# Last mixture of experts: each expert's slots past the first 256 under a branch on its token count

## The chip, the cores and the metric

The kernel runs on one core of one Trainium2 chip. A core has a matrix engine (PE, with its weight loads shown apart as PEld), a vector engine (DVE), a scalar engine (ACT), a general engine (POOL) and a queue engine (SP) that only issues transfers. Each engine runs its own instruction stream in order; the streams meet at semaphores. The metric is device microseconds of one execution, lower is better, as the median of three runs.

## The reference, cut to what matters

The model is four layers of graph attention or convolution, each followed by a feed-forward block, over 2708 nodes of 256 features. Only the last feed-forward block is touched. It is a switch-style mixture: every token goes to one of eight experts, an expert has a capacity of 424 slots, and tokens past the capacity are dropped.

```python
CAPACITY_FACTOR = 1.25
T = B * L                                   # 2708
C = max(1, math.ceil(CAPACITY_FACTOR * T / E))   # 424, E = 8
...
idx = jnp.argmax(probs, axis=-1)
pos = (jnp.cumsum(one_hot, axis=0) * one_hot).sum(-1).astype(jnp.int32) - 1
kept = pos < C
buf = jnp.zeros((E, C, D), dtype=h.dtype).at[idx, pos_safe].set(x, mode='drop')
hmid = jax.nn.relu(jnp.einsum('ecd,edf->ecf', buf, w1) + b1[:, None, :])
ybuf = jnp.einsum('ecf,efd->ecd', hmid, w2) + b2[:, None, :]
y_tok = ybuf[idx, pos_g] * (prb * kept)[:, None]
y = jnp.nan_to_num(y, nan=0.0, posinf=10000.0, neginf=-10000.0)
```

The slots of an expert are filled from 0 upwards in token order, so an expert with 211 tokens has slots 0 to 210 filled and 211 to 423 empty.

## The kernel before, in words

The kernel computes the four layers one after the other. Its last stage is the class `Switch`. While the last attention runs, `chunk` and `rank` compute the gate, each token's expert and its slot; `rank` is run in two parts, and `self.sofar` holds on every partition how many tokens each expert has got so far. `slots` then makes three tables from the slot numbers, each 128 partitions by 32 columns (8 experts times 4 tiles of 128 slots): `idg`, the row to fetch for a slot (row 0, which holds zeros, where the slot is empty), `ids`, the row to write (beyond the bounds where the slot is empty, so that nothing is written), and `prob`.

`experts` does the work, expert by expert:

- `gather` (L4749) fetches the expert's rows on POOL's queue by four indirect transfers into `xe`: 128, 128, 128 and 40 slots. Three `xe` buffers, so gathers run up to two experts ahead.
- SP loads `w1t` (L4767), `b1t`, `w2t` (L4771) and `b2t`, 2 MB of weights for each expert, into two sets of buffers.
- PE transposes `xe` in 128-column blocks into PSUM (`xt_ps`, L4778), and DVE (L99) and ACT (L101) in turn copy one half each to `xT`.
- PE computes the hidden layer for all 424 slots, in eight blocks of 128 hidden units (`h_ps`, L4788, three PSUM buffers); ACT adds the bias and applies the ReLU into `hT` (L4795). Every matmul is f32 and appears as two records in the trace.
- PE computes the output of each of the four tiles of slots (`y_ps`, L4800, eight hidden blocks, three PSUM buffers).
- DVE takes each output tile through nine operations (L4809 to L4818): bias, probability, three masks, three predicated copies for the NaN rule, and the residual.
- POOL writes the tile's rows to `out` by an indirect transfer (L4819).

The order of the instructions on each engine is made by the tile framework's scheduler from this program. It places the transposes of the next expert after the output tiles of the present one. After the last expert, `model` branches on `general` (L4956): a slow general path over the whole model that is taken only if the fast path met data that it can't treat. One branch of that kind stands in the third layer too (L4347), around a whole expert that may be unused; it is read on every engine from a one-element tile `used`. Where such a branch is not entered, each engine goes to a short second block which advances the semaphores by what the body would have given.

Of the kernel before, what the change touches and what calls it, by code (L numbers as in the profile page):

```python
# [8 lines left out]
F32 = mybir.dt.float32  # L9
I32 = mybir.dt.int32  # L10
U32 = mybir.dt.uint32
BF16 = mybir.dt.bfloat16
AF = mybir.ActivationFunctionType
ALU = mybir.AluOpType
# [4 lines left out]
N = 2708  # L19
D = 256  # L20
# [2864 lines left out]
class Route:  # L2885
# [10 lines left out]
    E = 8  # L2896
# [1114 lines left out]
class Deal:  # L4011
# [7 lines left out]
    T = (3, 2)  # L4019
# [415 lines left out]
class Switch:  # L4435
# [8 lines left out]
    E, HD, CAP = 8, 1024, 424  # L4444
    T = (CAP + 127) // 128
    S = E * T
    PARTS = 5

    def __init__(self, k, ctx, w, out, most):

        nc, tc = k.nc, k.tc
        E, S, T = self.E, self.S, self.T
        self.k, self.w, self.out, self.most = k, w, out, most
        keep = ctx.enter_context(tc.tile_pool(name="s3", bufs=1))
        self.dram = ctx.enter_context(tc.tile_pool(name="s3d", bufs=1, space=DRAM))
        self.fd = self.dram.tile([N + 1, 2 * D], F32, name="fd")
        self.idg = keep.tile([128, S], I32, name="idg")
        self.ids = keep.tile([128, S], I32, name="ids")
        self.prob = keep.tile([128, S], F32, name="prob")
        self.front = ExitStack()  # L4460
        pool = self.front.enter_context(tc.tile_pool(name="s3f", bufs=1))
        self.tmp = self.front.enter_context(tc.tile_pool(name="s3t", bufs=2))
        self.one = self.front.enter_context(tc.tile_pool(name="s3o", bufs=1))
        ps = self.front.enter_context(tc.tile_pool(name="ps_s3", bufs=1, space=PSUM))
        misc = ps.tile([128, 512], F32, name="misc_ps")
        n = self.PARTS * S
        self.id_ps = misc[:, :n]
        self.gl_ps = [misc[:, n + 32 * i : n + 32 * (i + 1)] for i in range(2)]
        n += 64
        self.tot_ps = misc[:, n : n + most * E]  # L4470
        self.in_ps = misc[:, n + most * E : n + 2 * most * E]
        assert n + 2 * most * E <= 512
        self.wg = pool.tile([128, 2, E], F32, name="wg")
        nc.sync.dma_start(self.wg, w["gate_w"].rearrange("(k p) e -> p k e", p=128))
        self.bg = pool.tile([128, E], F32, name="bg")
        nc.sync.dma_start(self.bg, brow(w["gate_b"], E))
        zero = pool.tile([1, 2 * D], F32, name="zero")
        nc.gpsimd.memset(zero, 0.0)
        nc.gpsimd.dma_start(self.fd[0:1, :], zero)
        self.lg = pool.tile([128, NT, E], F32, name="lg")  # L4480
        nc.gpsimd.memset(self.lg, 0.0)

        def count(name, n, step, **kw):
            t = pool.tile([128, n], F32, name=name)
            nc.gpsimd.iota(
                t,
                [[step, n]],
                channel_multiplier=kw.get("mult", 0),
                base=kw.get("base", 0),
                allow_small_or_imprecise_dtypes=True,  # L4490
            )
# [19 lines left out]
        self.every = pool.tile([128, 128], F32, name="every")  # L4511
        nc.gpsimd.memset(self.every, 1.0)
        self.later = pool.tile([128, E, most], F32, name="later")
        nc.gpsimd.memset(self.later, 1.0)
        nc.gpsimd.memset(self.later[:, :, 0:1], 0.0)

        self.valid = pool.tile([128, NT], F32, name="valid")
        nc.vector.tensor_scalar(self.valid, self.own, float(N), None, ALU.is_lt)
        self.p1 = pool.tile([128, 1], F32, name="p1")
        nc.vector.tensor_scalar(self.p1, self.own[:, 0:1], 1.0, None, ALU.add)  # L4520
        self.slot_f = pool.tile([128, 1 + self.PARTS, S], F32, name="slot_f")
        self.sofar = pool.tile([128, E], F32, name="sofar")
        nc.vector.memset(self.sofar, 0.0)
# [185 lines left out]
    def slots(self):  # L4709

        nc, S = self.k.nc, self.S
# [8 lines left out]
        v.tensor_copy(self.ids, idf)  # L4720
        v.tensor_tensor(self.prob, f[:, 3, :], f[:, 4, :], ALU.add)
        v.tensor_tensor(self.prob, self.prob, f[:, 5, :], ALU.add)
        self.front.close()

    def experts(self):
# [6 lines left out]
        with ExitStack() as ctx:  # L4732
# [25 lines left out]
                    )  # L4758
                return xe

            nxt = gather(0)
            for e in range(E):
                xe = nxt
                if e + 1 < E:
                    nxt = gather(e + 1)
                w1t = wp.tile([128, 2, HD], F32, name="w1t")
                nc.sync.dma_start(w1t, w["w1"][e].rearrange("(k p) h -> p k h", p=128))  # L4767
                b1t = wp.tile([128, M], F32, name="b1t")
# [2 lines left out]
                nc.sync.dma_start(w2t, w["w2"][e].rearrange("(m p) d -> p m d", p=128))  # L4771
                b2t = wp.tile([128, D], F32, name="b2t")
                nc.sync.dma_start(b2t, brow(w["b2"][e], D))
                xT = dp.tile([128, 2, CAP], F32, name="xT")
                for kk in range(2):
                    tp = pst.tile([128, CAP], F32, name="xt_ps")
                    for i, (o, n) in enumerate(tiles):
                        nc.tensor.transpose(  # L4778
                            tp[:, o : o + n],
                            xe[:n, i, kk * 128 : (kk + 1) * 128],  # L4780
                            k.ident[:n, :n],
                        )
                    k.copy(xT[:, kk, :], tp)
                hT = dp.tile([128, M, CAP], F32, name="hT")
                for m in range(M):
                    hp = ps1.tile([128, CAP], F32, name="h_ps")
                    for kk in range(2):
                        nc.tensor.matmul(  # L4788
                            hp,
                            lhsT=w1t[:, kk, m * 128 : (m + 1) * 128],  # L4790
                            rhs=xT[:, kk, :],
                            start=(kk == 0),
                            stop=(kk == 1),
                        )
                    nc.scalar.activation(hT[:, m, :], hp, AF.Relu, bias=b1t[:, m : m + 1])  # L4795
                for i, (o, n) in enumerate(tiles):
                    c = e * T + i
                    y = ps2.tile([128, D], F32, name="y_ps")
                    for m in range(M):
                        nc.tensor.matmul(  # L4800
                            y[:n],
                            lhsT=hT[:, m, o : o + n],
                            rhs=w2t[:, m, :],
                            start=(m == 0),
                            stop=(m == M - 1),
                        )

                    g = op.tile([128, D], F32, name="g")
                    nc.vector.tensor_tensor(g[:n], y[:n], b2t[:n], ALU.add)  # L4809
                    nc.vector.tensor_scalar(g[:n], g[:n], prob[:n, c : c + 1], None, ALU.mult)  # L4810
                    big = 3.4028234e38
                    mask = op.tile([128, 3, D], I32, name="mask")
                    nc.vector.tensor_tensor(mask[:n, 0, :], g[:n], g[:n], ALU.not_equal)
                    nc.vector.tensor_scalar(mask[:n, 1, :], g[:n], big, None, ALU.is_gt)
                    nc.vector.tensor_scalar(mask[:n, 2, :], g[:n], -big, None, ALU.is_lt)
                    for q in range(3):
                        nc.vector.copy_predicated(g[:n], mask[:n, q, :], sub[:n, q, :])
                    nc.vector.tensor_tensor(g[:n], g[:n], xe[:n, i, D:], ALU.add)  # L4818
                    nc.gpsimd.indirect_dma_start(  # L4819
                        out=out,  # L4820
                        out_offset=bass.IndirectOffsetOnAxis(
                            ap=ids[:n, c : c + 1], axis=0
                        ),
                        in_=g[:n],
                        in_offset=None,
                        bounds_check=N - 1,
                        oob_is_err=False,
                    )


def any_model(tc, I, out):
# [175 lines left out]
```

## Time and profile before

| | us |
|---|---|
| median of three runs (2376.36 to 2380.46) | 2378.51 |
| the profiled execution's own time | 2375.75 |
| span of the profiled execution | 2374.0 |
| PE busy in the span | 2225.6 (94%) |
| DVE busy in the span | 1537.0 (65%) |
| ACT busy in the span | 701.4 (30%) |
| POOL busy in the span | 423.3 (18%) |

The groups of instructions of the last stage, by line, between 2121 us and the end (busy time of the group, number of records):

| line | engine, what | records | busy us |
|---|---|---|---|
| L4788 | PE, hidden layer, 128x424 | 256 | 95.7 |
| L4800 | PE, output, 128 slots by 256 | 384 | 84.2 |
| L4800 | PE, output, 40 slots by 256 | 128 | 29.2 |
| L4778 | PE, transposes, 128 and 40 rows | 64 | 14.0 |
| L4795 | ACT, bias and ReLU, 128x424 | 64 | 39.3 |
| L4749 | POOL, gathers | 32 | 32.4 |
| L4819 | POOL, scatters | 32 | 31.8 |

The time that is compared is that of whole executions; the trace is one execution. Busy time of PE is the sum of matmul records, whose ends are modelled; how long a stage lasts is better read from where its first records start.

### The profile page before, as it was taken

How to read it: one execution, taken by the hardware profiler on the slowest of the kernel's cores; microseconds unless marked ns; L12 is line 12 of the kernel's file. 1: busy time of each engine (PE TensorE's matmuls, PEld its weight loads, DVE VectorE, ACT ScalarE, POOL GpSimd, SP SyncE). 2: the span in 40 equal slices, each digit the busy share in tenths (PEclk: the TensorE clock that was granted, in tenths of full speed). 3: DMA queues.
4: the chain of work that ended last, by engine and by line, in shares of the span. 5: the costliest groups of instructions: out<-in, count | busy, mean ns of one | idle time of the engine just before them, and what ended most of it. 6: DMA issues, size and time to landing. Idle time of an engine off the chain costs nothing. (4 is left out here: it accounts for less than half of the span.)

```text
span 2374.0 us, 32068 instructions
## 1 busy us (share of the span) xinstructions
PE 2225.6 (94%) x11600; PEld 1486.7 (63%) x11600; DVE 1537.0 (65%) x3478; ACT 701.4 (30%) x1469; POOL 423.3 (18%) x451
## 2 busy tenths in 40 slices
PE   7999999988899999999879998999999999959996
PEld 4777765577778767777668886667632333326664
DVE  7588887745676656655665646363589998844444
ACT  6433333213656222221150103134541211211220
POOL 1100013003100134556300010523100000012321
PEclk9999999969999999999989996999999999979998
DMA  5244332110657144333245554113133433323330
GB/s 152 67 113 114 111 85 84 38 38 12 220 158 227 42 128 100 77 83 54 31 151 150 149 165 90 23 52 97 43 97 107 114 113 102 87 101 130 125 117 15
DMA packets 168113, 235.25 MB, mean 99 GB/s; under 512 B 32126, under 2 KB 101476, under 8 KB 167941
## 3 DMA queue, kind: packets, MB, share of 16 engines
q1 hardware_dynamic: 130320, 184.03, 26.9%
q0 software_dynamic: 18688, 32.97, 6.2%
q10 hardware_dynamic: 18932, 16.05, 2.1%
q8 instruction: 96, 1.57, 0.3%
q14 instruction: 77, 0.62, 0.1%
HBM read 200.31 MB, written 33.74 MB: 99 GB/s over the span
## 5 line engine op out<-in xcount | busy, mean ns | idle before, releaser
L3551 DVE SCALAR_TENSOR_TENSOR PT<-Rr,Q,aj 128x512 f32<-128x512 f32 (+3 forms) x630 | 395.5, 680 | 103.9 <-PE acc_ps L3650 79.6
L3725 PE MATMUL acc_ps<-PT,V 128*64 128x512 f32 (+4 forms) x2016 | 333.7, 551 | 0.0
L3725 PEld LDWEIGHTS acc_ps<-PT,V 128*64 128x64 f32 (+1 forms) x2016 | 94.2, 123 | 210.2 <-issue 159.1
L1845 PE MATMUL acc_ps<-fa,PT 128*128 128x257 f32 x882 | 215.4, 383 | 1.2 <-DVE out L1865 1.2
L1845 PEld LDWEIGHTS acc_ps<-fa,PT 128*128 128x128 f32 x882 | 164.0, 190 | 66.4 <-issue 33.8
L3650 PE MATMUL acc_ps<-V,PT 128*128 128x257 f32 x882 | 196.6, 384 | 1.7 <-issue 1.6
L3650 PEld LDWEIGHTS acc_ps<-V,PT 128*128 128x128 f32 x882 | 167.9, 192 | 29.3 <-issue 2.5
L3305 PE MATMUL h_ps<-xT,w1t 128*128 128x384 f32 x512 | 176.9, 499 | 3.5 <-ACT xT L3296 3.5
L3322 PE MATMUL y_ps<-w2t,hT 128*128 128x256 f32 x768 | 169.8, 380 | 0.0
L2512 PE MATMUL acc_ps<-V,at 128*128 128x257 bf16 x1323 | 158.3, 278 | 9.2 <-DVE at L2503 7.4
L3322 PEld LDWEIGHTS y_ps<-w2t,hT 128*128 128x128 f32 x768 | 145.0, 190 | 21.0
L2512 PEld LDWEIGHTS <-at 128*128 128x128 bf16 x1323 | 129.6, 100 | 33.0 <-issue 5.2
L3305 PEld LDWEIGHTS h_ps<-xT,w1t 128*128 128x128 f32 x512 | 96.1, 193 | 68.3 <-ACT xT L3296 8.5
L1817 ACT ACTIVATE PT<-s_ps,rq 128x512 f32<-128x512 f32 (+1 forms) x126 | 79.5, 636 | 174.4 <-PE s_ps L1793 168.8
L3334 POOL DMA_INDIRECT acc<-ys,ids x48 | 91.7, 1911 | 156.9 <-DVE ys L3331 125.3
L1793 PE MATMUL s_ps<-KT,QT 128*128 128x512 f32 (+1 forms) x252 | 116.2, 548 | 2.5 <-ACT PT L1817 1.6
L1818 DVE SCALAR_TENSOR_TENSOR PT<-aj,PT 128x512 f32<-128x512 int32 (+1 forms) x126 | 79.2, 633 | 57.8 <-ACT PT L1817 57.5
L3004 POOL DMA_INDIRECT xe<-fd,idg x48 | 79.6, 1659 | 195.6 <-DVE early_f L3035 181.2
L4800 PE MATMUL y_ps<-w2t,hT 128*128 128x256 f32 (+1 forms) x512 | 112.8, 380 | 0.0
L3330 DVE TENSOR_TENSOR ys<-y_ps,b2t 128x256 f32<-128x256 f32 x48 | 20.3, 423 | 136.4 <-PE y_ps L3322 136.4
L3312 ACT ACTIVATE hT<-h_ps,b1t 128x384 f32<-128x384 f32 x128 | 74.2, 580 | 115.3 <-PE h_ps L3305 115.3
L4749 POOL DMA_INDIRECT xe<-fd,idg x32 | 32.4, 1013 | 411.4 <-DVE ids L4720 402.1
(795 smaller groups left out, 3538.8 us busy)
## 6 DMA issues: line engine op xcount, KB each, us to landing
aj<-in_adjT SPq DMA_DIRECT2D x399, 256.0 KB, 2.7
w1t<-in_L_ffn_W SPq DMA_DIRECT2D x8, 1024.0 KB, 5.2
w2t<-in_L_ffn_W SPq DMA_DIRECT2D x8, 1024.0 KB, 5.8
w1t<-in_L_ffn_w SPq DMA_DIRECT2D x8, 1024.0 KB, 6.9
w2t<-in_L_ffn_w SPq DMA_DIRECT2D x8, 1024.0 KB, 5.6
fd<-fa ACTq DMA_DIRECT2D x13, 512.0 KB, 3.1
aj<-in_adjT SPq DMA_DIRECT2D x63, 74.0 KB, 2.1
aj<-in_adjT SPq DMA_DIRECT2D x21, 202.0 KB, 2.4
```

The costliest lines, as they stand in the source:

```text
L1793: nc.tensor.matmul(s[:, :cs], lhsT=QT[:, j * 128 : j * 128 + 128], rhs=KT[:, c0 : c0 + cs], start=True, stop=True,)
L1817: nc.scalar.activation(PT[p, :n], s[p, :n], AF.Exp, scale=r)
L1845: nc.tensor.matmul(ac, lhsT=PT[:, o : o + n], rhs=fa[:, j, :], start=j == 0, stop=False)
L2512: nc.tensor.matmul(ac[:, c:], lhsT=at[:, o : o + n], rhs=V[:, j, r], start=j == 0 and q == 0, stop=False, skip_group_check=True,)
L3004: nc.gpsimd.indirect_dma_start(out=xe[:, i, :], out_offset=None, in_=self.fd[:rows, :], in_offset=bass.IndirectOffsetOnAxis(ap=idx[:, i : ...
L3305: nc.tensor.matmul(hp, lhsT=w1t[:, kk, m * 128 : (m + 1) * 128], rhs=self.xT[:, kk, :], start=(kk == 0), stop=(kk == 1),)
L3322: nc.tensor.matmul(y, lhsT=self.hT[:, m, i * 128 : (i + 1) * 128], rhs=w2t[:, m, :], start=(m == 0), stop=(m == M - 1),)
L3334: add = nc.gpsimd.indirect_dma_start(out=acc, out_offset=bass.IndirectOffsetOnAxis(ap=self.ids[:, i : i + 1], axis=0), in_=ys, in_offset=None,
L3551: nc.vector.scalar_tensor_tensor(PT, R, Q, aj, ALU.max, ALU.mult)
L3650: nc.tensor.matmul(ac[:n], lhsT=PT[:, o : o + n], rhs=V[:, j, 0, :], start=(j == 0), stop=False,)
L3725: nc.tensor.matmul(w.pop("out"), **w)
L4800: nc.tensor.matmul(y[:n], lhsT=hT[:, m, o : o + n], rhs=w2t[:, m, :], start=(m == 0), stop=(m == M - 1),)
```

## The change

Expert `e`'s work is split by slot tiles into `ahead` (tiles 0 and 1, 256 slots) and `rest` (tiles 2 and 3, 168 slots). Transposes, hidden layer and outputs of `ahead` run always. The hidden layer and the outputs of `rest` stand under a branch that is entered if the expert has more than 256 tokens. The counts are compared once for all experts, in `slots`. All four tiles are still gathered and transposed, and all weights are loaded. The flag of the branch is the count's comparison plus a number that is always zero, computed from the finished first output tile, so that it exists only once that tile is through DVE.

```diff
+    FIRST = 2
...
+        self.more = keep.tile([128, E], F32, name="more")
...
+        v.tensor_scalar(self.more, self.sofar, 128.0 * self.FIRST, None, ALU.is_gt)
         self.front.close()
...
-            nxt = gather(0)
-            for e in range(E):
-                xe = nxt
-                if e + 1 < E:
-                    nxt = gather(e + 1)
+            def load(e):
...
+            def turn(xe, xT, ts):
+                o0, o1 = ts[0][1], ts[-1][1] + ts[-1][2]
                 for kk in range(2):
-                    tp = pst.tile([128, CAP], F32, name="xt_ps")
-                    for i, (o, n) in enumerate(tiles):
+                    tp = pst.tile([128, 256], F32, name="xt_ps")
+                    for i, o, n in ts:
...
-                    k.copy(xT[:, kk, :], tp)
+                    k.copy(xT[:, kk, o0:o1], tp[:, : o1 - o0])
+
+            def up(wt, xT, hT, ts):
...
                 for m in range(M):
-                    hp = ps1.tile([128, CAP], F32, name="h_ps")
+                    hp = ps1.tile([128, 256], F32, name="h_ps")[:, : o1 - o0]
...
+            def down(e, wt, xe, hT, i, o, n):
...
+            ts = [(i, o, n) for i, (o, n) in enumerate(tiles)]
+            ahead, rest = ts[: self.FIRST], ts[self.FIRST :]
+
+            def begin(e):
+                xe, wt = gather(e), load(e)
+                return xe, wt, dp.tile([128, 2, CAP], F32, name="xT")
+
+            nxt = begin(0)
+            turn(nxt[0], nxt[2], ahead)
+            for e in range(E):
+                xe, wt, xT = nxt
+                hT = dp.tile([128, M, CAP], F32, name="hT")
+                up(wt, xT, hT, ahead)
+                turn(xe, xT, rest)
+                if e + 1 < E:
+                    nxt = begin(e + 1)
+                    turn(nxt[0], nxt[2], ahead)
+                used = op.tile([1, 1], I32, name="used")
+                for i, o, n in ahead:
+                    g = down(e, wt, xe, hT, i, o, n)
+                    if i == 0:
+
+                        no = op.tile([1, 1], F32, name="no")
+                        nc.vector.tensor_tensor(no, g[:1, :1], g[:1, :1], ALU.is_lt)
+                        nc.vector.tensor_tensor(
+                            used, self.more[:1, e : e + 1], no, ALU.add
                         )
+                with tc.If(nc.values_load(used, min_val=0, max_val=1)):
+                    up(wt, xT, hT, rest)
+                    for i, o, n in rest:
+                        down(e, wt, xe, hT, i, o, n)
```

`up` and `down` hold the loops of before (hidden layer with its activation; output tile with its nine DVE operations and its scatter), over the tiles that they are given.

More of the change, by code (lines that the diff above doesn't have):

```diff
@@ L4773, in experts @@
                 nc.sync.dma_start(b2t, brow(w["b2"][e], D))
-                xT = dp.tile([128, 2, CAP], F32, name="xT")
+                return w1t, b1t, w2t, b2t
+            def turn(xe, xT, ts):
+                o0, o1 = ts[0][1], ts[-1][1] + ts[-1][2]
                 for kk in range(2):
-                    tp = pst.tile([128, CAP], F32, name="xt_ps")
-                    for i, (o, n) in enumerate(tiles):
+                    tp = pst.tile([128, 256], F32, name="xt_ps")
+                    for i, o, n in ts:
                         nc.tensor.transpose(
-                            tp[:, o : o + n],
+                            tp[:, o - o0 : o - o0 + n],
                             xe[:n, i, kk * 128 : (kk + 1) * 128],
@@ L4782, in experts @@
                         )
-                    k.copy(xT[:, kk, :], tp)
-                hT = dp.tile([128, M, CAP], F32, name="hT")
+                    k.copy(xT[:, kk, o0:o1], tp[:, : o1 - o0])
+            def up(wt, xT, hT, ts):
+                w1t, b1t, _, _ = wt
+                o0, o1 = ts[0][1], ts[-1][1] + ts[-1][2]
                 for m in range(M):
-                    hp = ps1.tile([128, CAP], F32, name="h_ps")
+                    hp = ps1.tile([128, 256], F32, name="h_ps")[:, : o1 - o0]
                     for kk in range(2):
@@ L4790, in experts @@
                             lhsT=w1t[:, kk, m * 128 : (m + 1) * 128],
[L4791 removed]
+                            rhs=xT[:, kk, o0:o1],
                             start=(kk == 0),
@@ L4794, in experts @@
                         )
[L4795 to L4805, printed above, removed]
-                        )
[L4808 to L4828, printed above, removed]
@@ new lines, in up @@
+                    nc.scalar.activation(
+                        hT[:, m, o0:o1], hp, AF.Relu, bias=b1t[:, m : m + 1]
+                    )
+            def down(e, wt, xe, hT, i, o, n):
+                _, _, w2t, b2t = wt
+                c = e * T + i
+                y = ps2.tile([128, D], F32, name="y_ps")
+                for m in range(M):
+                    nc.tensor.matmul(
+                        y[:n],
+                        lhsT=hT[:, m, o : o + n],
+                        rhs=w2t[:, m, :],
+                        start=(m == 0),
+                        stop=(m == M - 1),
+                    )
+                g = op.tile([128, D], F32, name="g")
+                nc.vector.tensor_tensor(g[:n], y[:n], b2t[:n], ALU.add)
+                nc.vector.tensor_scalar(g[:n], g[:n], prob[:n, c : c + 1], None, ALU.mult)
+                big = 3.4028234e38
+                mask = op.tile([128, 3, D], I32, name="mask")
+                nc.vector.tensor_tensor(mask[:n, 0, :], g[:n], g[:n], ALU.not_equal)
+                nc.vector.tensor_scalar(mask[:n, 1, :], g[:n], big, None, ALU.is_gt)
+                nc.vector.tensor_scalar(mask[:n, 2, :], g[:n], -big, None, ALU.is_lt)
+                for q in range(3):
+                    nc.vector.copy_predicated(g[:n], mask[:n, q, :], sub[:n, q, :])
+                nc.vector.tensor_tensor(g[:n], g[:n], xe[:n, i, D:], ALU.add)
+                nc.gpsimd.indirect_dma_start(
+                    out=out,
+                    out_offset=bass.IndirectOffsetOnAxis(ap=ids[:n, c : c + 1], axis=0),
+                    in_=g[:n],
+                    in_offset=None,
+                    bounds_check=N - 1,
+                    oob_is_err=False,
+                )
+                return g
```

## The prediction

> **What bounds the kernel now.** I read the page's engine table first (PE busy 94%), then the stage that the change touches: the table by stretches of the last 253 us, the chain that ended last, the timeline, then the transfers. Stretch table (length; busy us and count of PE, PEld, DVE, ACT, POOL; clock; DMA share; GB/s), one expert and the end:
>
> ```profile
> 2193.00:2220.00 27.00, 26.90 (x106) 17.78 (x105) 13.73 (x38) 5.42 (x9) 8.00 (x9) 1.00 0.40 126
> 2355.00:2374.00 19.00, 0.00 (x0) 0.00 (x0) 2.66 (x8) 0.00 (x0) 2.14 (x2) 0.56 0.02 7
> ```
>
> PE fills the expert's 27 us; DVE is half idle, DMA 40% busy. The chain (start, length) repeats one pattern for each expert:
>
> ```profile
> 2193.61 11.65 PE h_ps L4788 x32
> 2205.26 13.94 PE y_ps L4800 x64
> 2219.20 0.68 PE xt_ps L4778 x4
> 2219.97 0.61 DVE xT L99
> 2220.62 11.65 PE h_ps L4788 x32
> ```
>
> So an expert lasts 2220.62 - 2193.61 = 27.01 us, of it 1.42 from the last output to the next hidden layer. What PE drops here comes off the end one for one, as long as nothing else becomes late. The first expert lasts longer (2137.27 to 2166.60 = 29.33), since its hidden layer takes 14.10 us after an idle stretch at clock 0.50. Durations that I need (timeline):
>
> ```profile
> 2178.09 14.10 PE L4800 MATMUL y_ps<-w2t,hT 128*128 128x256 f32 x64
> 2181.74 0.42 DVE L4809 TENSOR_TENSOR g<-y_ps,b2t 128x256 f32<-128x256 f32 x1 [11.92 <-PE y_ps L4800]
> 2185.25 0.42 DVE L4809 TENSOR_TENSOR g<-y_ps,b2t 128x256 f32<-128x256 f32 x1
> 1685.30 2.18 PE L4261 MATMUL h_ps<-fT,w1t 128*128 128x148 f32 x16
> ```
>
> A 256-column record costs 14.10/64 = 0.220 us, one output tile (16 records) 3.52; a 148-column record with the same weight size 0.136; DVE takes a tile through in about 3.55.
>
> **Which experts skip.** The trace tells: a scatter of tile 2 moves bytes only for filled slots. These are the software queue's lines (packets, MB, share of the engines) in the stretches in which tile 2 of experts 0, 1 and 3 was written:
>
> ```profile
> q0 software_dynamic: 48, 0.00, 0.4%
> ...
> q0 software_dynamic: 48, 0.04, 2.1%
> ...
> q0 software_dynamic: 48, 0.13, 6.5%
> ```
>
> 0.13 MB is a full tile (128 rows of 1 KB). The same view gives 0.00 for experts 2 and 4 as well, 0.13 for 5 and 6, and 0.07 for 7. So experts 0, 2 and 4 have nothing past slot 255: three of eight skip.
>
> **What a branch costs.** The kernel has two already. L4347 and L4956 are both not entered (min/median/max ns):
>
> ```profile
> L4347 PEldq TENSOR_LOAD <-used x1: 487/487/487, 1578.4 to 1578.4; - x1
> L4347 PEldq COMPARE_BRANCH  x1: 3670/3670/3670, 1579.0 to 1579.0; - x1
> L4347 ACTq COMPARE_BRANCH  x1: 50/50/50, 1574.9 to 1574.9; - x1
> L4347 DVEq COMPARE_BRANCH  x1: 72/72/72, 1581.8 to 1581.8; - x1
> L4956 PEldq COMPARE_BRANCH  x1: 3637/3637/3637, 2351.1 to 2351.1; - x1
> L4956 POOLq INC_SWDGE_SEM  x1: 2087/2087/2087, 2362.9 to 2362.9; - x1
> 1582.84 0.30 PE L4361 MATMUL xt_ps<-ident,xe 128*128 128x128 f32 x1 [2.08 <-PEq L4347]
> ```
>
> PE's jump costs 3.65 us where it passes over much code (by L4347's shapes 22 token tiles, over 1,000 PE instructions); ACT and DVE, passing over some 48, pay 0.05 to 0.07. The register load at 1578.4 ran while PE was still in the outputs (to 1580.5): the sequencer works ahead of the array.
>
> [...] here 2.08 us of idleness at 1582 left the next matmuls at full speed, and the first expert shows the slow start.
>
> **The change, part by part.** From the changed program's instruction order and the semaphores that each instruction names. t is time from the first hidden matmul of an expert.
>
> Always: hidden layer of 256 slots, 32 x 0.220 = 7.05; two output tiles 7.05; t = 14.10. Then PE's transposes: four for the next expert's tiles 2 and 3, and four for tiles 0 and 1 of the one after that. (The scheduler runs transposes one expert further ahead, so the next hidden layer never waits for a copy behind the branch.) First four: 4 x 0.174 (8 took 1.39) = 0.70. The others wait for ACT's and DVE's copies out of the two `xt_ps` buffers. DVE: tile 0 arrives at 10.6, done at 14.3; `no` 0.14 (the 1x1 `used` at L4008 took 0.14); first operation of tile 1, 0.42; `used`, about 15.1; its copy to 15.45. So PE ends its transposes near 16.1, against 15.5 without these waits. The register load starts when the last transpose is handed over: 15.75 + 0.49 = 16.2, branch 0.05.
>
> Not entered: the second block's semaphore step and jump, 0.2 (at L4347 the matmul followed 0.17 after the branch): next expert at 16.5. Saves 27.0 - 16.5 = 10.5 each for experts 2 and 4. DVE still finishes tile 1 (to 18.5) and POOL its 2.09 us semaphore step; both lie under the next expert's 14 us before anyone asks for them.
>
> Entered: hidden layer of 168 slots, 32 records; by columns 0.141 (424 take 0.356), floor 0.136; I take 0.148: 4.73; outputs 7.05. 16.35 + 4.73 + 7.05 = 28.15, so +1.15 each for 1, 3, 5. DVE's tail of tile 3 is covered: the next `h_ps` buffers wait for ACT alone, and ACT's first copy waits for PE only. If that cover failed it would cost up to 3.6 each.
>
> Ends: expert 0: 7.05 + 2.72 (slow start, 14.10 - 32 x 0.356) + 0.70 (four transposes before its outputs) + 7.05 + 2.4 + 0.25 (five semaphore waits of 0.05 ahead of the first branch) = 20.2: saves 9.1. Expert 6 has four transposes fewer: +0.55. Expert 7 has none, but PE waits for `used`: branch over at 15.7, outputs end at 27.5 against 25.6: +1.9. `more` is one DVE operation of 128x8, 0.17, before the first gather: +0.1.
>
> Sum: -9.1 - 21.0 + 3.45 + 0.55 + 1.9 + 0.1 = **-24.1**. Profiled execution 2375.75 becomes 2351.7; it lies 2.8 under the median shown, so the median becomes **2354.4**.
>
> Moved queues: SP's load of the expert two on is now issued after the branch, when PE has freed the buffers: near the start of the expert before it. Landing took 6.5 to 6.9 (w1t), 5.6 (w2t), together some 12, against 16.5: hidden. POOL's gather for the expert two on comes after the branch too: from t = 5.2 (after a skip, behind its 2.09) or 7.5 (after an entered branch, behind a scatter that waits for the landing of the one before, 5.9 at most). Its second tile is asked for at 15.4, issued at 6.5 or 8.8; gathers landed in 4.4 in the median, some 7 in the loaded start: about 2 spare, costing nothing.
>
> **Unknown: PE's short jump.** The body is 32 matmuls of the program, 128 PE instructions with weight loads. No jump of that size on PE is in the trace. Below: 0.05 as on ACT; above: 3.65, plus up to 2.7 if the clock drops. I take 0.05[...]; a gain is excluded. The range keeps the other end.
>
> **Rivals.**
> - *Skips refetch on PE* (22%): one to three of the skips cost 3.65: 2358 to 2365, with the clock 2373. For: both PE jumps in the trace cost it. Against: both were far.
> - *Late gathers* (4%): PE waits at the transposes; a landing of 10 us gives five waits of 1 to 3.4: near 2364.
> - *Every branch refetches, entered or not* (6%), the slower side: place, PE at all eight branches; price 3.65 each, 29.2 - 24.1 = +5.1: 2383.6, more if the clock drops. It decides from 3.0 us per branch. Against: L4347's final jump within PE's code cost 0.17 with its semaphore step.
> - *Flag always set* (3%): no skip, eight entered: 1.15 x 6 + 0.55 + 1.9 + 0.4 = +9.7: 2388. Against: `sofar` is complete before `slots`, and the trace shows three experts at or under 256.
>
> **How the numbers follow.** Likeliest as worked out: 60%, 2350 to 2359 with the terms' spread; 5% stays for other causes. 0.2% (4.8 us) is what this measurement can tell. Faster: 60 + 22 + 4 and 2 of the rest, 88%. Within: 3%. Slower: 6 + 3, 9%. Range 2349 to 2367: from three us better terms to three skips with a refetch and some more.
>
> **What would show it.** Hidden-layer starts 16.5 us apart after experts 2 and 4 and 28.2 after 1, 3 and 5; 160 records of the 168-column hidden layer, five experts' worth; PE's compare-and-branch under 0.1 us. Wrong if these branches read 3.6, if PE idles over 1 us at a transpose for `xe`, or if 256 such records appear.

## The result, and the profile after

| | before | after |
|---|---|---|
| median, us | 2378.10 (2376.36 to 2380.46) | 2341.39 (2338.96 to 2347.69) |
| profiled execution, us | 2375.75 | 2339.33 |
| its span, us | 2374.0 | 2337.5 |

The ratio is 0.9849, with a 95% interval of 0.9826 to 0.9872: faster by 36.7 us, where 24 were forecast and the range ended at 29.5. (The kernel before has four runs here; the table ahead of the prediction had three of them, with the median 2378.51.) The direction and the mechanism were right, the size was not. Three experts skip their branch, that is, PE jumps over its body, as was read from the bytes of the scatters. The groups by line and shape of the last stage (records, then busy us, mean ns, idle time before them and its releasers) have 160 hidden-layer records of 168 columns, five experts' worth:

```profile
L4793 PE MATMUL h_ps<-xT,w1t 128*128 128x256 f32 x256 | 59.8, 394 | 1.8 <-PEq L4865 1.8
L4793 PE MATMUL h_ps<-xT,w1t 128*128 128x168 f32 x160 | 24.1, 309 | 1.9 <-DVE g L4819 1.9
```

The table by stretches (length; busy us and count of PE, PEld, DVE, ACT, POOL; clock; DMA share; GB/s), for expert 2 (skips), expert 3 (enters), and from the last output to the end:

```profile
2177.45:2193.75 16.30, 15.48 (x74) 13.08 (x73) 9.09 (x29) 4.21 (x10) 7.01 (x7) 1.00 0.45 132
2193.75:2221.23 27.48, 27.09 (x137) 22.33 (x137) 12.44 (x35) 7.79 (x19) 7.09 (x7) 1.00 0.50 168
...
2319.46:2337.50 18.04, 0.00 (x1) 0.00 (x0) 3.35 (x10) 0.00 (x0) 1.91 (x2) 0.60 0.02 7
```

PE still bounds an expert: 15.48 of 16.30 us busy in a skipped one. The chain that ended last (start, length) through expert 5, which enters, has a copy by ACT in the middle of the transposes, where a copy by DVE stood behind them before:

```profile
2237.51 7.15 PE h_ps L4793 x32
2244.66 6.91 PE y_ps L4809 x32
2251.57 0.75 PE xt_ps L4780 x4
2252.34 0.31 ACT xT L101
2252.69 0.66 PE xt_ps L4780 x4
2253.35 4.70 PE h_ps L4793 x32
2258.05 7.03 PE y_ps L4809 x32
2265.08 7.10 PE h_ps L4793 x32
```

No branch stands in this chain: PE's second hidden layer follows the transposes at once. Where a branch does cost, the timeline shows it as idle time before the instruction that follows (in brackets, with the releaser). First the skip of expert 2, then the entry of expert 7, which has no transposes to fill the wait:

```profile
2192.66 0.66 PE L4780 MATMUL xt_ps<-ident,xe 128*128 128x128 f32 x4 [0.39 <-ACT xT L101]
2193.75 2.61 PE L4793 MATMUL h_ps<-xT,w1t 128*128 128x256 f32 x11 [0.43 <-PEq L4865]
...
2307.61 4.68 PE L4793 MATMUL h_ps<-xT,w1t 128*128 128x168 f32 x31 [1.33 <-DVE g L4819]
```

The branch's own instructions on PE at expert 2 (ns, then start) show a jump of 0.36 us; the general branch after the last expert took 3.64 us before and 3.74 after:

```profile
L4865 PEldq TENSOR_LOAD <-used x1: 304/304/304, 2192.7 to 2192.7; - x1
L4865 PEldq COMPARE_BRANCH  x1: 364/364/364, 2193.1 to 2193.1; - x1
```

The prediction took everything ahead of the first hidden matmul as unchanged. It isn't. These are PE's timelines of the start, first before, then after:

```profile
2133.19 0.43 PE L4778 MATMUL xt_ps<-ident,xe 40*128 40x40 f32 x2 [0.24 <-DMA xe<-fd,idg]
2136.72 0.45 PE L4778 MATMUL xt_ps<-ident,xe 128*128 128x128 f32 x1 [3.10 <-DMA xe<-fd,idg]
2137.27 3.17 PE L4788 MATMUL h_ps<-xT,w1t 128*128 128x424 f32 x4
```

```profile
2124.44 0.66 PE L4780 MATMUL xt_ps<-ident,xe 128*128 128x128 f32 x2 [7.12 <-DMA xe<-fd,idg]
2127.02 0.69 PE L4780 MATMUL xt_ps<-ident,xe 128*128 128x128 f32 x2 [1.92 <-DMA xe<-fd,idg]
2129.12 1.02 PE L4780 MATMUL xt_ps<-ident,xe 128*128 128x128 f32 x4 [1.41 <-DMA xe<-fd,idg]
2130.12 3.33 PE L4793 MATMUL h_ps<-xT,w1t 128*128 128x256 f32 x7
```

Before, a ninth transpose stands ahead of expert 0's hidden layer, and it waits 3.10 us for a gather: it is expert 1's. So the order described for the kernel before, in which the next expert's transposes follow the outputs, does not hold for this one. After, it stands behind the hidden layer. From the first gather (2121.85 before, 2118.23 after) to the first hidden matmul it is 15.42 us before and 11.89 after.

To see which part belongs to the change, each trace is cut at four points: first gather, first hidden matmul, end of the last output, end of the span. (An expert's period, below, is the time from its first hidden matmul to that of the next expert, for the last one to the end of its outputs.) The experiments give two more traces of the changed kernel and one more of the kernel before (us; the last column is the position of the first gather):

| kernel | start | experts | end | sum | first gather |
|---|---|---|---|---|---|
| before | 15.42 | 216.99 | 19.74 | 252.15 | 2121.85 |
| before again (e8) | 14.90 | 217.37 | 19.82 | 252.09 | 2119.71 |
| after | 11.89 | 189.34 | 18.04 | 219.27 | 2118.23 |
| after again (e1) | 12.16 | 188.71 | 18.14 | 219.01 | 2152.49 |
| after, third (e9) | 12.50 | 188.40 | 18.21 | 219.11 | 2143.49 |
| no branch (e3) | 12.34 | 216.18 | 19.38 | 247.90 | 2154.30 |
| all entered (e5) | 12.69 | 222.97 | 18.37 | 254.03 | 2120.97 |

The sums repeat within 0.3 us, so the change is worth 252.1 - 219.1 = 33.0 us: about 3.0 at the start, 28.4 in the experts, 1.65 at the end. The other 3.6 us between the two profiled executions lie ahead of the first gather, where the programs' work is the same but for the comparison of the counts, 0.16 us on DVE.

### The profile page after: what moved, and what is told of

Its sections match the earlier page's. It is cut to its first block, busy times and chain, and to the rows that moved or that the text cites. A ratio compares the mean times of both kernels' runs of the same rounds, so it can differ in the third digit from the quotient of the medians.

```text
span 2337.5 us, 32378 instructions
## 1 busy us (share of the span) xinstructions
PE 2188.8 (94%) x11664; PEld 1493.0 (64%) x11664; DVE 1519.2 (65%) x3449; ACT 709.3 (30%) x1517; POOL 417.5 (18%) x445
## 3 DMA queue, kind: packets, MB, share of 16 engines
q1 hardware_dynamic: 130320, 184.03, 27.5%
## 5 line engine op out<-in xcount | busy, mean ns | idle before, releaser
L4278 PE MATMUL y_ps<-w2t,hT 128*128 128x256 f32 (+1 forms) x432 | 99.5, 379 | 0.0
```

The source lines that it names most:

```text
L4278: last = nc.tensor.matmul(y[:n], lhsT=hT[:, m, o : o + n], rhs=wts[e][1][:, m, :], start=(m == 0), stop=(m == M - 1),)
```

## The experiments

Runs sent together share a chip and its runs of the kernel before, so ratios are compared, not microseconds: on the chip of e1 to e4 and that of e9 to e12 the kernel before took 2405 to 2406, on that of e5 to e8 2375.5.

**e1: the changed kernel again.**

> The changed kernel as it is, once more. Theory: of the 36.5 us between the two profiles only the stage from its first gather to its last output belongs to the change (about 31: 27.6 in the experts' periods, 3.4 in the start of expert 0); the 3.6 us by which the first gather came earlier and the 2 us after the last output are this execution's own. Then in this trace first gather to first hidden matmul is 11.9, first hidden matmul to the end of the outputs 189.3, each within 0.4, while the first gather may stand anywhere between 2118 and 2124, and five rounds give a gain of 29 to 35. Rival: the change makes the untouched stages faster, by where the code lies; then the first gather stands at 2118.2 again, within 0.7, and the gain is 36 to 37.

Measured: 2371.62 against 2405.06, ratio 0.9861 (0.9844 to 0.9878), 33.4 us. Start 12.16, experts 188.71 (expected 189.3 within 0.4, so 0.2 beyond). The first gather stood at 2152.49, far outside the expected window, because this chip is slower as a whole, so the expectation's test by position says nothing. But e1 and e4, whose work ahead of it is the same, differ there by 4.4 us on one chip. So the 3.6 us can be an execution's own, and the sum of the stage agrees with the measured gain. The shorter end, which the expectation took for chance, was there again (18.14): it belongs to the program.

**e2: the kernel before, with expert 1's transposes behind expert 0's hidden layer.**

```diff
-                            k.ident[:n, :n],
+                            (late if e == 1 else k.ident)[:n, :n],
...
+                if e == 0:
+                    late = dp.tile([128, 128], F32, name="late")
+                    no = op.tile([128, 1], F32, name="no")
+                    nc.vector.tensor_tensor(no, hT[:, M - 1, :1], hT[:, M - 1, :1], ALU.is_lt)
+                    nc.vector.tensor_scalar(late, k.ident, no, None, ALU.add)
```

> The kernel before, with expert 1's transposes made to follow expert 0's hidden layer (two small vector operations give their identity matrix a dependence on it). Theory: in the kernel before one transpose of expert 1, which waits for its gather, stands ahead of expert 0's hidden layer and holds it for 3.1 us; then first gather to first hidden matmul falls from 15.4 to 12.0 to 12.3, all later periods stay at 27.0, expert 0's at 29.3 to 29.6, and the time falls by 3 (ratio 0.9987). Rival: the landing of the first weights (15.2 us in the table of transfers) holds the hidden layer; then 15.2 to 15.4 stays and the time is unchanged.

Measured: ratio 0.9990 (0.9981 to 0.9999); start 13.10, where 12.0 to 12.3 was expected. From the timeline:

```profile
2164.86 0.43 PE L4778 MATMUL xt_ps<-ident,xe 40*128 40x40 f32 x2 [0.49 <-DMA xe<-fd,idg]
2165.38 0.51 ACT L101 COPY xT<-xt_ps 128x424 f32<-128x424 f32 x1 [22.42 <-PE xt_ps L4778]
2165.93 14.58 PE L4788 MATMUL h_ps<-xT,w1t 128*128 128x424 f32 x32 [0.63 <-issue]
```

The hidden layer no longer waits for expert 1, and not for its weights either: it starts as the second copy to `xT` ends (2165.89). The start fell by 1.8 to 2.3 of the 3 us. Most of what is left is the gap of 0.63 after the last transpose, in which the 424-column copies run. With the split hidden layer this gap is gone: it needs only tiles 0 and 1, which are copied while tiles 2 and 3 are transposed. Expert 0's period rose to 29.87, so the stage gained 2.1 in sum.

**e3: the split without a branch.**

```diff
-                with tc.If(nc.values_load(used, min_val=0, max_val=1)):
-                    up(wt, xT, hT, rest)
-                    for i, o, n in rest:
-                        down(e, wt, xe, hT, i, o, n)
+                up(wt, xT, hT, rest)
+                for i, o, n in rest:
+                    down(e, wt, xe, hT, i, o, n)
```

> The changed kernel with the rest of each expert's slots run always, with no branch and no flag in the program. Theory: the start is as in the changed kernel (11.9), splitting the hidden layer costs 0.1 to 0.2 for each expert, so periods of 27.1 to 27.3 and expert 0 at 29.3; in all 1 to 3 us under the kernel before (2375 to 2377). Rival: the start in the changed kernel came from the branch (its queue of semaphores or the moved transfers), then it is 15.4 here and the time is 1 above before; or the split hidden layer is what costs the 0.5 of an entered expert, then periods are 27.5.

Measured: 2403.77 against 2405.06, ratio 0.9990 (0.9981 to 0.9998); by the trace 4.2 us under the kernel before from the first gather on. Start 12.34: the start's gain needs the split and the order, not a branch. The periods of experts 1 to 6 are 26.96 to 26.98, no longer than before (27.01): splitting a hidden layer of 424 columns into 256 and 168 costs next to nothing (from its first record to the next step's, 7.01 and 4.56 us here, 11.49 in one). Expert 0 took 27.74 instead of 29.3 to 29.7, and expert 7 26.60 instead of 25.59: four transposes lie in expert 0's period instead of seven, and four in expert 7's instead of none. The timeline shows how the transposes lie here:

```profile
2201.39 0.90 PE L4780 MATMUL xt_ps<-ident,xe 128*128 128x128 f32 x4
2202.22 0.70 PE L4809 MATMUL y_ps<-w2t,hT 128*128 128x256 f32 x2
2202.75 0.60 PE L4780 MATMUL xt_ps<-ident,xe 128*128 128x128 f32 x4
2203.19 6.64 PE L4809 MATMUL y_ps<-w2t,hT 128*128 128x256 f32 x30
```

**e4: the flag without its wait.**

```diff
+            flags = [
+                nc.values_load(self.more[:1, e : e + 1], min_val=0, max_val=1)
+                for e in range(E)
+            ]
...
-                with tc.If(nc.values_load(used, min_val=0, max_val=1)):
+                with tc.If(flags[e]):
```

`more` becomes an integer table, and `no` and `used` go. The scheduler still places each register load right ahead of its branch.

> The changed kernel with the flag read straight from the table of counts, without the number that waits for the finished first output tile. Theory: that wait costs only where no transposes stand behind the outputs, at expert 7 (1.3 us of idle PE ahead of its second hidden layer); that one goes to 0.1 or less, skips stay at 16.3 and entered experts at 27.5, in all 1.2 under the changed kernel. Rival: PE's wait at all branches is for the flag; then skips fall to 15.9, entered experts to 27.3, expert 0 by 0.7, and the sum is 3 to 4.

Measured: ratio 0.9858 (0.9843 to 0.9873). Skips 16.32 and 16.29, entered 27.48 to 27.50: no change there. Expert 7 fell from 27.26 to 25.67 and expert 6 from 27.20 to 26.53. The second hidden layer of expert 7 starts without a wait:

```profile
2335.15 4.72 PE L4793 MATMUL h_ps<-xT,w1t 128*128 128x168 f32 x32
```

So the wait for the flag cost 1.6 + 0.7 = 2.3 us, where few or no transposes stand between the outputs and the branch; I had missed expert 6. As whole runs, 1.6 us between e4 and e1 is within their spread.

**e5: all experts enter.**

```diff
-        v.tensor_scalar(self.more, self.sofar, 128.0 * self.FIRST, None, ALU.is_gt)
+        v.tensor_scalar(self.more, self.sofar, -1.0, None, ALU.is_gt)
```

> The changed kernel with the comparison always true (counts over minus one), so that all eight experts take the branch. Theory: an entered branch costs 0.5 against the same program without it (27.5 against 26.97 between hidden layers), expert 7 0.7 and expert 0 about 2 (its branch has five more semaphore waits); experts 0, 2 and 4 rise by 11.2 each over the changed kernel, so the stage from the first hidden matmul to the last output lasts 222 (216.2 without a branch, 188.7 in the changed kernel), and against the kernel before the time is within 2 us of no change: plus 5 in the stage, minus 3.3 at its start, minus 1.7 after its last output. Rival: the whole gain is not in the skipped work but in the new order and start; then this stays 10 or more under the kernel before.

Measured: 2378.07 against 2375.5, ratio 1.0007 (0.9998 to 1.0016); experts 222.97. Periods: 30.82 for expert 0, 27.52 to 27.56 for experts 1 to 5, 27.20 for 6, and 27.26 for 7. With nothing to skip the change gains nothing. Against e3 the eight branches, with the order of the transposes that goes with them, cost 222.97 - 216.18 = 6.8 us.

**e6: a second branch, around tile 3.** On the kernel of e4:

```diff
+        v.tensor_scalar(self.full, self.sofar, 384.0, None, ALU.is_gt)
...
                     up(wt, xT, hT, rest)
-                    for i, o, n in rest:
-                        down(e, wt, xe, hT, i, o, n)
+                    down(e, wt, xe, hT, *rest[0])
+                    with tc.If(nc.values_load(self.full[:1, e : e + 1], min_val=0, max_val=1)):
+                        down(e, wt, xe, hT, *rest[1])
```

> The changed kernel with the flag read from the table of counts and, inside the branch, a second branch around the output of tile 3, taken if the expert has more than 384 tokens. By the scatters' bytes expert 7 has no slots there, expert 1 hardly any. Theory: each expert without them saves 3.5 of PE and its share of DVE, the inner branch's register load runs ahead while PE is in tile 2, so it costs 0.3 or less in experts 3, 5 and 6: 6 to 7 under the kernel with the early flag alone, 8 to 9 under the changed kernel, ratio 0.982 against before. Rival: an inner branch stops PE's run-ahead and costs 1 us or more each in five experts; then 1 to 3.

Measured: 2337.97 against 2375.5, ratio 0.9843 (0.9829 to 0.9857), 37.5 us, the most together with e11. The experts fell to 180.54, 6.0 under e4: expert 1 to 24.55, expert 7 to 22.10, both skipping tile 3, while 3 and 5 stayed at 27.5. But the end grew from 17.7 to 19.83, so that from the first gather to the end it is 3.8 under e4, where 6 to 7 was expected. Its last lines of PE and POOL:

```profile
2313.05 3.62 PE L4811 MATMUL y_ps<-w2t,hT 128*128 128x256 f32 x16
2320.56 0.98 POOL L4830 DMA_INDIRECT out_x<-g,ids  x1 [6.96 <-DVEq L4866]
```

After expert 7's skip POOL still runs its semaphore step, 1.90 us, now with nothing behind which it could hide. Two of the six microseconds went there.

**e7: a longer body.** The second hidden layer is computed seven times.

```diff
-                    up(wt, xT, hT, rest)
+                    for _ in range(7):
+                        up(wt, xT, hT, rest)
```

> The changed kernel with the second hidden layer in the branch written seven times (512 PE instructions in the body in place of 128; entered experts are longer by 28 us each, which is not compared). Theory: PE's jump costs by how far it goes; with 512 instructions passed over [...] its compare-and-branch reads 3.5 to 3.8 at experts 0, 2 and 4, and the hidden layer that follows a skip comes 3.3 to 3.6 later (periods of experts 2 and 4 19.6 to 19.9). Rival: the 3.65 belongs to the two general branches alone (thousands of instructions), then 16.3 stays and the branch reads under 0.4.

One execution, of which only the trace is read. Measured: the three skips' jumps on PE took 3.51, 3.84 and 3.53 us, and the periods of experts 2 and 4 became 19.77 and 19.48. Expert 2's branch, in the timeline the hidden layer behind it, and the stretch of that layer (columns as above; the clock is the third number from the end):

```profile
L4865 PEldq COMPARE_BRANCH  x1: 3837/3837/3837, 2227.6 to 2227.6; - x1
```

```profile
2231.75 8.75 PE L4793 MATMUL h_ps<-xT,w1t 128*128 128x256 f32 x32 [3.90 <-PEq L4865]
2231.75:2240.50 8.75, 8.75 (x33) 7.47 (x34) 0.32 (x1) 3.55 (x8) 4.05 (x4) 0.81 0.91 299
```

The rival "skips refetch on PE" was a matter of size: a jump over 128 PE instructions costs 0.24 to 0.36 here, over 512 as much as the general branches' 3.64 and 3.74. The two traces of the pair have one packet of 16 KB on the instruction queue (q8) within each of PE's three long jumps (1579.0 to 1582.7 and 2351.1 to 2354.7 before, 2316.5 to 2320.2 after) and none within expert 2's skip (2193.1 to 2193.5); that the jump waits for it is not shown. And the jump is not its whole price: in the three hidden layers that follow a skip (experts 1, 3 and 5) the granted clock was 0.72, 0.81 and 0.71, and they took 9.85, 8.75 and 10.01 us, where the changed kernel takes 7.14 at clock 1.00. Had the body been that long, it would have taken back 3.2 to 3.5 us at experts 2 and 4 each, and 1.6 to 2.9 more in the expert behind each skip.

**e8: the kernel before again.**

> The kernel before once more, for its trace. Theory: what the changed kernels show after their last output (17.7 to 18.1 us to the end) belongs to the program, so here it is 19.7 again within 0.3, POOL's last drain 7.79 in place of 7.30; and the position of the first gather varies from execution to execution in the same program, so it stands 1 us or more away from 2121.85. Rival: both are chance; then the end lasts anything between 17.7 and 19.7.

Measured: end 19.82, first gather at 2119.71, 2.1 from the first trace, start 14.90 with expert 1's transpose waiting 1.91. The same program's position ahead of the stage varies by more than half of the 3.6 us, and the end by 0.1. POOL's last drain (ns: least, median, longest) before, after, in e5 (nothing skipped) and in e6 (eight scatters skipped):

```profile
L5003 POOLq DRAIN  x3: 46/170/7790, 2365.0 to 2373.7; - x3
```

```profile
L5043 POOLq DRAIN  x3: 46/103/7297, 2329.4 to 2337.2; - x3
```

```profile
L5043 POOLq DRAIN  x3: 46/103/7792, 2366.4 to 2374.7; - x3
```

```profile
L5042 POOLq DRAIN  x3: 46/103/7133, 2328.6 to 2336.3; - x3
```

The longest one is 7.79, 7.30, 7.79 and 7.13 with 0, 6, 0 and 8 scatters left out: 0.082 us for each.

**e9: the changed kernel, third time.**

> The changed kernel a third time, on the chip of the next runs, as their measure. Theory: as before, first gather to first hidden matmul 11.9 to 12.9, stage from there to the last output 188.7 to 189.4, gain 33 within 4.

Measured: 2373.60 against 2405.72, ratio 0.9868 (0.9846 to 0.9891), 32.1 us. Start 12.50; experts 188.40, 0.3 under what was expected.

**e10: room for four halves.**

```diff
-                for kk in range(2):
-                    tp = pst.tile([128, 256], F32, name="xt_ps")
+                both = pst.tile([128, 2, 256], F32, name="xt_ps")
+                for kk in range(2):
+                    tp = both[:, kk, :]
```

> The changed kernel with both halves of a transposed block in one PSUM tile, so that four halves can wait for their copies in place of two. Theory: the 0.5 by which an entered expert is longer than one without a branch in the program (27.50 against 26.97) is PE's wait of 0.39 at the fifth transpose for a copy, and not the branch; with four halves that wait goes and the periods fall to 27.1 (entered) and 15.9 (skipped), some 2.5 under the changed kernel over the stage. Rival: PE must wait for the flag or the register load anyway, which come at the same time; then PE stops at the branch instead and the periods stay.

Measured: 2378.78, ratio 0.9880 (0.9860 to 0.9900), 5 us above e9; the experts took 193.85 instead of 188.4. The theory fell. The entered periods of experts 3 and 5 came to 27.38 and 27.41, only 0.1 shorter, and the skips grew to 16.80 and 17.36. The scheduler spread the transposes differently, and PE now waits for a gather and at the branch (expert 2's skip, timeline; below it expert 1's hidden layer, as timeline and as stretch):

```profile
2233.70 0.69 PE L4781 MATMUL xt_ps<-ident,xe 128*128 128x128 f32 x2 [0.33 <-DMA xe<-fd,idg]
2235.21 7.14 PE L4794 MATMUL h_ps<-xT,w1t 128*128 128x256 f32 x32 [0.83 <-PEq L4866]
...
2189.33 8.83 PE L4794 MATMUL h_ps<-xT,w1t 128*128 128x256 f32 x32 [1.08 <-PEq L4866]
2189.33:2198.16 8.83, 8.83 (x34) 7.44 (x35) 1.11 (x4) 3.31 (x7) 5.04 (x5) 0.81 0.93 306
```

So of the copy's 0.39 only 0.1 was a cost of its own, and e4 had shown that the flag alone costs an entered expert nothing: the two waits end at nearly the same time. With both gone, in e11 below, experts 3 and 5 take 27.26. Of the 5.4 us of loss against e9, 2.3 lie in expert 0 (21.15; 0.9 of it in its slow start), 1.6 in the two skips and 1.6 in expert 1 (29.08). The last comes with the clock: expert 1's hidden layer ran at a granted clock of 0.81 and took 8.83 us instead of 7.14, behind a wait of 1.08 us. The same stands in e11 and e12, behind waits of 1.11 and 1.06; in e9, with 1.06, the clock stayed at 1.00. What decides it was not tested.

**e11: e6 and e10 together.**

> The kernel with the early flag and the inner branch around tile 3, with both halves of a transposed block in one PSUM tile besides. Theory: the stage falls from 180.5 to 178, so 8 to 10 under the changed kernel on the same chip, ratio 0.981 to 0.983 against the kernel before; after the last output it stays at 19.8, since POOL's semaphore step of the skipped inner branch (1.9) stands at the end of the program. POOL's last drain reads 7.13 again if it goes by the number of scatters run (8 left out). Rival: the wait is replaced by one at the branch and the stage stays at 180.

Measured: 2367.67 against 2405.72, ratio 0.9830 (0.9805 to 0.9855). Experts 182.50, where 178 was expected and e6 took 180.54. Of the 2 us, 1.7 is expert 1's hidden layer at clock 0.81 (8.83 us); besides it, experts 0 and 4 grew and the entered 3 and 5 shrank (27.26 from 27.5), to about nothing in sum. End 19.67; last drain 7.13 again. With e6 this is the best ratio, 5.9 us under e9 on the same chip; their intervals overlap at the edge (0.9855 and 0.9846). By the sums of the traces (first gather to end) e6 is 6.4 and e11 4.6 under the changed kernel.

**e12: expert 1's transposes asked for early.**

```diff
-                up(wt, xT, hT, ahead)
-                turn(xe, xT, rest)
-                if e + 1 < E:
+                if e == 0:
+                    turn(xe, xT, rest)
+                    nxt = begin(e + 1)
+                    turn(nxt[0], nxt[2], ahead)
+                up(wt, xT, hT, ahead)
+                if e > 0:
+                    turn(xe, xT, rest)
+                if 0 < e < E - 1:
```

> The changed kernel with expert 1's first transposes asked for ahead of expert 0's hidden layer (the scheduler puts two of them after its first block and two after the first matmul of its second). Theory: PE's order alone sets the start; PE now waits inside expert 0's hidden layer for expert 1's gather, 1 to 3 us, so that the first hidden matmul still comes 11.9 to 12.9 after the first gather and expert 0's outputs 1 to 3 later than in the changed kernel (its period 20.5 to 22.5, in place of 19.1 to 19.8). Rival: gathers of expert 1 have landed by then; the period stays.

One execution, of which only the trace is read. Measured: start 12.15 as expected; but the waits inside expert 0's hidden layer came to 0.37 and 0.18, not to 1 to 3 us, and its period to 19.82, against 18.89 to 19.81 in the three traces of the changed kernel. So the place of the transposes sets the start, and behind the first matmuls they cost little. Expert 1's period, 29.18, is long by the clock, as said at e10. The timeline inside expert 0's hidden layer:

```profile
2166.72 0.66 PE L4780 MATMUL xt_ps<-ident,xe 128*128 128x128 f32 x2 [0.37 <-DMA xe<-fd,idg]
2167.17 0.96 PE L4793 MATMUL h_ps<-xT,w1t 128*128 128x256 f32 x2
2168.32 0.44 PE L4780 MATMUL xt_ps<-ident,xe 128*128 128x128 f32 x2 [0.18 <-issue]
```

Expert 1's first transpose came 14.57 us after the first gather, where it comes in the kernel before too (14.87 and 14.35). The landing is the same; what changed is what PE does until then.

## Why the prediction was right and wrong

Right: which experts skip; that PE's time falls off the end one for one; that transfers and gathers moved behind the branch stay hidden (no wait for weights or for `xe` appears in the changed kernel past expert 0); that the jump over 128 instructions is nearer to 0.05 than to 3.65. The forecast for a skip was 16.5, and 16.3 came, in part by luck. The register load was expected from t = 15.75 to 16.2; at expert 2 it ran from 15.2 to 15.5. The jump was put at 0.05, an estimate from ACT's branch of 0.05 over some 48 instructions, and took 0.36, over the 0.1 that the prediction named as its sign, and the step behind it at 0.2 and took 0.3. The errors offset each other but for 0.2.

Wrong, by terms (traces of the changed kernel against the two of the kernel before; us):

| term | predicted | measured |
|---|---|---|
| ahead of the first hidden matmul | 0 | -3.0 |
| expert 0 | -9.1 | -10.3 (-9.7 to -10.6) |
| experts 2 and 4, each | -10.5 | -10.7 |
| experts 1, 3, 5, each | +1.15 | +0.5 |
| expert 6 | +0.55 | +0.2 |
| expert 7 | +1.9 | +1.7 |
| after the last output | 0 | -1.65 |

**The start** is the largest step that failed: the prediction put everything ahead of the first hidden matmul at nothing. The text spoke of transposes that run "one expert further ahead" and charged expert 0 with four of them ahead of its outputs, but never asked where they stood before. One of them stood ahead of the hidden layer and waited for a gather. e2 takes that transpose away in the kernel before (15.2 to 13.1), and e3 shows the rest to come with the split (12.3), both without a branch.

**Expert 0** gained 1.2 more than forecast. Its slow start was put at 2.72; from the 11.65 of the prediction's own chain it is 14.10 - 11.65 = 2.45. In the changed kernel the hidden layer took 9.69, 8.95 and 8.70 us, so 1.5 to 2.5 over the 7.17 of expert 2's at clock 1.00 (the granted clock in it was 0.73 in the first of these traces, 0.82 in the last).

**Entered experts** were priced at a register load that starts late (t = 15.75) and is 0.49 us long, read from L4347; the other load of that trace, at L4956, took 0.31. In the new branch it takes 0.30, starts at 15.2, and ends under the transposes: the second hidden layer starts at t = 15.7, not 16.35. That is 0.65 in each of three experts, some 2 us, and part of expert 6's. What remains of 0.5 is the branch with its neighbours: e3 without one has 26.97. Without the copy's wait it is 0.4 (e10), without the flag's still 0.5 (e4), without both 0.3 (e11, which has the inner branch besides). How that 0.3 divides between the register load, the jumps and the order of the transposes is open.

**The end** was taken as fixed. It is 1.65 shorter: POOL's last drain 0.49 and its semaphore step at the general branch 0.13 (2.087 to 1.956), and some 1 us in POOL's jump there (3.3 to 3.4 us from compare to first semaphore in the four traces of programs without the new branches, 2.5 to 2.8 in all those with them) and in the closing steps. The first two go with the number of scatters run (the step took 2.08 to 2.09, 1.96 and 1.91 us with 0, 6 and 8 left out); why the jump is shorter was not tested.

These errors make 9 us (3.0 + 4.2 + 1.65), and all have one sign. None of them alone leaves the range: with the start put right the forecast would have been 27.1 us, with all of them it is 33.0, past the range's end at 29.5. The last 3.6 us of the profiled pair aren't the change's: the three measured ratios give 36.7, 33.4 and 32.1 us, around the 33.0 of the traces.

Of the rivals, "flag always set" was forecast at +9.7; e5 forces it and measures +1.7 (-0.5 to +3.8), since the start, the end and the cheaper entry are in it. "Skips refetch" needed a longer body (e7), and the slower clock that the prediction added to it came there too, by 1.6 to 2.9 us against its "up to 2.7". In the trace of before, PE's granted clock was 1.00 behind the 2.08 us of idleness at the third layer's branch (1582.84 to 1590.00); in e10 to e12 a fall to 0.81 followed waits of 1.06 to 1.11 us, so it can follow a skip even with a short jump. "Late gathers" and "every branch refetches" did not occur.

## What to carry to other kernels

A branch on data gives back what it skips, less the jump of the engine that sets the end: 0.24 to 0.36 us here over 128 instructions, and ten times that over 512 (3.51 to 3.84), with a slower clock behind it (0.71 to 0.81). Work of the next item between the last result and the branch lets the flag and the register load end under it (entered experts took 27.5 us with the flag's wait and without it); where nothing stands there (the last item) the wait is bare (1.33 us ahead of expert 7's second hidden layer). When a restructuring reorders an engine's stream, list for each instruction that moves the place that it leaves as well as the place it goes to: something queued behind it may have been waiting for its inputs (3.10 us here). And of two waits that end together, the removal of one is worth next to nothing (0 and 0.1 of 0.5 us here).

## What the runs showed of the hardware

POOL's last drain fell by 0.082 us for each indirect scatter that was not run, in 14 traces with three counts left out (0, 6 and 8: 7.79, 7.30 and 7.13 us). A PE jump over 512 instructions took 3.5 to 3.8 us (e7), one over 128 0.24 to 0.36 (changed kernel), with the same flag and the same engines. PE's granted clock was lower behind the long jumps' waits of 3.6 to 4.2 us (hidden layers of 8.75 to 10.01 us at clock 0.71 to 0.81, e7), and in three other traces behind waits of only 1.06 to 1.11 us (8.83 us at 0.81, e10 to e12), while e9 kept 1.00 behind one of 1.06 and the kernel before 1.00 behind one of 2.08. POOL's semaphore step after a skipped block took 1.1 to 1.9 us, which is hidden inside the stage and bare at the end of the program (1.90 us, e6).
